# A new begin for two Gram stages: ten pixel groups transposed by TensorE, the centre subtracted behind them, a half step of transfers first

## The chip, the cores and the metric

The kernel runs on one core of a Trainium2 chip. The metric is the device time of one execution in microseconds (us), as the median of several runs. Smaller is better.

## What is computed

The reference applies two bottleneck layers, one after the other, to x of shape 64 x 1024 x 14 x 14 in float32. Cut to what matters, one layer is:

```python
def _bn(x, gamma, beta):
    mean = jnp.mean(x, axis=(0, 2, 3), keepdims=True)
    var = jnp.var(x, axis=(0, 2, 3), keepdims=True)
    xn = (x - mean) * jax.lax.rsqrt(var + EPS)
    return gamma.reshape(1, -1, 1, 1) * xn + beta.reshape(1, -1, 1, 1)

out = relu(_bn(_conv(x, w1, b1, 1, 0), g1, be1))      # 1x1, 1024 -> 256 channels
out = relu(_bn(_conv(out, w2, b2, 1, 1), g2, be2))    # 3x3, 256 -> 256
out = _bn(_conv(out, w3, b3, 1, 0), g3, be3)          # 1x1, 256 -> 1024
out = softplus(residual_scale)[0] * out
return relu(x + out)
```

The mean and variance of each `_bn` run over all 64 images and 196 pixels, 12544 pixels in all. So a layer needs the statistics of its third convolution before it can finish the first pixel.

## The kernel before

**Layout.** The 256 channels in the middle lie as 128 partitions times 2 slots (`s`). `y_all` holds the output of the second convolution for all 12544 pixels (`NPX`) in SBUF.

**Stages.** A layer (block `b` = 0, 1) runs the first convolution, then the second, then a Gram stage, then the third convolution with the residual. In block 0 the third convolution is interleaved with block 1's first.

**The Gram stage.** The third convolution is linear, so the mean and variance of its 1024 outputs follow from the mean and the matrix of second moments of its 256 inputs. The function `gram` builds that matrix. Products of pixels with pixels need the pixels on the partitions, so each group of 256 pixels (`CH * P`, 49 groups) is first transposed into a tile `zt` (six of them in rotation). Then TensorE multiplies the group with itself: two halves of 128 pixels, four products each, added up in two banks of PSUM (`cp`, `ap`; line L170, as all matmuls). The products of a group are queued on TensorE behind the transposition of the next one.

**Two ways to transpose.** `by_tensor` lets TensorE do it: four passes against the identity into PSUM (L1075), then VectorE copies the result to `zt` (L1082). `by_vector` uses VectorE's transpose of 32x32 blocks (L1089). For that the pixels are first brought into another order by transfers: `spread(k)` moves a step of 1536 pixels (`STEP`) from `y_all` into one of two tiles, `homes`, by twelve transfers of 96 KB (L1067), seven issued by SyncE's queue (SP) and five by GpSimd's (POOL). `stay(k)` copies the four diagonal parts on ScalarE (L333). A step makes six groups. A home can be filled again only when VectorE has read the step in it. In block 0 the first home is the tile `ws`, which later holds the sums of weights.

**What is done to y before.** The second batch norm and its ReLU are applied in place, in pieces, by ScalarE (`norm`, through the helper at L333); one small piece goes to VectorE instead (`norm_vector`, L552 and L554). Then VectorE subtracts a constant of each channel, so that the products stay small (`less`, L1033; `minus_c` holds the negated constant). Both must be over before a group is transposed or a step is moved. The order of ScalarE, VectorE and TensorE is the order of the program wherever `keep_in_program_order` is used, which is so for all that is named here, except for two of the four additions in a `combine`.

**Order before.** `FIRST = 7` groups go through TensorE. Step 0 is moved after the second of them, step 1 after the sixth. Seven steps of six groups by VectorE follow; after step k, `spread(k + 2)` is issued, later pieces are normalized and centred, and `stay(k + 2)` is queued. The dummy matmul `busy(psum, "ax", 1)` behind the first group, and seven of them ahead of the stage, keep TensorE's clock up.

**After the groups.** `combine_w3` (and `combine_w1` in block 0) make sums of weights on VectorE, four additions of 512 columns each (L150 to L153), behind the last group's transposition. `conv3_stats` turns the matrix into the statistics; its tile `q` is its own, and `by_mean` lies in the second home (`spare`).

Of the kernel before, what the change touches and what calls it, by code (L numbers as in the profile page):

```python
# [37 lines left out]
FP = mybir.dt.float32  # L38
AF = mybir.ActivationFunctionType
ALU = mybir.AluOpType  # L40

P = 128
# [13 lines left out]

Q = P // 2

FIRST, LAST = 7, 0
RUN = 3 * P  # L60
STEP = 4 * RUN
STEPS = (NPX - (FIRST + LAST) * CH * P) // STEP

LAG = 14

# [24 lines left out]
def bottlenecks(ctx: ExitStack, tc: tile.TileContext, x, w1s, w2s, w3s, pars, out):  # L90
# [240 lines left out]
    def act(*args, **kw):  # L331

        tc.keep_in_program_order(nc.scalar.activation(*args, **kw))  # L333
# [221 lines left out]

    def conv2(psum, pool, b, par, aff, affine_of, stats):

# [438 lines left out]
    def gram(psum, pool, homes, aff, minus_c, beside):  # L996
# [27 lines left out]
        ):  # L1024
            nc.gpsimd.memset(by[i][here, cols], value)

        head = 3 * CH * P
        start = FIRST * CH * P
        bounds = [0, CH * P, head, head + STEP, *range(2 * GPX, NPX + 1, GPX)]
        pieces = list(zip(bounds, bounds[1:]))  # L1030

        def less(s, y):
            tc.keep_in_program_order(nc.vector.tensor_scalar(y, y, minus_c[:, s : s + 1], None, ALU.add))  # L1033

        def norm_to(end):

            while pieces and pieces[0][0] < end:
                a, e = pieces.pop(0)
                for s in reversed(range(MS)):
                    y = y_all[:, s, a:e]  # L1040
                    if a == 0 and s == 1:
                        norm_vector(s, y, aff, minus_c[:, s : s + 1])
                    else:
                        norm(s, y, aff, act)
                        less(s, y)

        def home(k):
            return homes[k % 2][:, : MS * STEP].rearrange("p (s j f) -> p s j f", s=MS, j=4)

        def first_of(k):  # L1050
            return start + k * STEP if k else head

        def stay(k):

            for i in range(4):
                here, a = slice(32 * i, 32 * i + 32), first_of(k) + i * RUN
                act(home(k)[here, :, i], y_all[here, :, a : a + RUN], AF.Copy)

        def spread(k):

            first = first_of(k)
            norm_to(first + STEP)
            x = home(k)
            for n, (i, j) in enumerate(itertools.permutations(range(4), 2)):
                queue = nc.gpsimd if n in (1, 3, 6, 8, 10) else nc.sync
                a = first + i * RUN
                queue.dma_start(out=x[32 * i : 32 * i + 32, :, j], in_=y_all[32 * j : 32 * j + 32, :, a : a + RUN])  # L1067
            return x.rearrange("p s j f -> p (s j) f")

        def by_tensor(a):  # L1070
            tp = psum.tile(CH * M)
            for c in range(CH):
                for s in range(MS):
                    tc.keep_in_program_order(
                        nc.tensor.transpose(  # L1075
                            tp[:, (c * MS + s) * P : (c * MS + s + 1) * P],
                            y_all[:, s, a + c * P : a + (c + 1) * P], ident,
                        )
                    )
            zt = next(zts)  # L1080
            tc.keep_in_program_order(
                nc.vector.tensor_copy(zt[:, :, 1 : M + 1], tp.rearrange("p (c m) -> p c m", c=CH))  # L1082
            )
            return zt

        def by_vector(x, i):
            zt = next(zts)
            tc.keep_in_program_order(
                nc.vector.transpose(  # L1089
                    zt[:, :, 1 : M + 1].rearrange("p b (n c) -> p b n c", c=32),  # L1090
                    x[:, :, i * CH * 32 : (i + 1) * CH * 32].rearrange("p n (b r) -> p b n r", r=32),
                )
            )
            return zt

        def pairs():

            norm_to(head)
            then = {
                1: lambda: ready.append(spread(0)),  # L1100
                2: lambda: (norm_to(2 * GPX), stay(0)),
                4: partial(norm_to, 3 * GPX),
                5: lambda: (ready.append(spread(1)), stay(1)),
            }
            for i in range(FIRST):
                a = i * CH * P
                yield by_tensor(a if a < head else a + STEP)
                if i == 0:
                    busy(psum, "ax", 1)
                if i in then:  # L1110
                    then[i]()
            for k in range(STEPS):
                x = ready.pop(0)
                for i in range(RUN // (CH * 32)):
                    yield by_vector(x, i)
                if k + 2 < STEPS:
                    ready.append(spread(k + 2))
                    norm_to(first_of(k + 2) + 2 * STEP)
                    stay(k + 2)
            norm_to(NPX)  # L1120
            for i in range(LAST):
                yield by_tensor(NPX - (LAST - i) * CH * P)

        ready = []
# [22 lines left out]
    def conv3_stats(psum, one, grams, w3, mv, tags, spare):  # L1147
# [277 lines left out]
    for b in range(2):  # L1425
# [7 lines left out]
        with tc.tile_pool(name=f"last_{b}", bufs=1) as one, tc.tile_pool(  # L1433
            name=f"last_x_{b}", bufs=4 if b == 0 else 5
        ) as xpool:
            w3 = load_w3(one, b)
            if b == 0:
                w1 = load_w1(one, b + 1, nc.sync)
            aff = affine(aggregate(stats2, 0), pb, G2, BE2)
            with ExitStack() as scope:  # L1440
                if b == 0:
                    psum = Psum(scope, ["cy", "ay", "cx", "cy", "ay"], cy=2, ay=2)
                else:
                    psum = Psum(scope, ["cy", "cx"], cy=2, cx=2, cp=2)
                with tc.tile_pool(name=f"gram_{b}", bufs=1) as pool:
                    def x_tile(name):
                        return xpool.tile([P, CS * PX], FP, tag="x", name=name)


                    ws = sums_tile(one, 2 - b)  # L1450
                    homes = [x_tile("home") if b else ws.rearrange("p i n -> p (i n)"), x_tile("home")]

                    weights = []

                    def combined():
                        if b == 0:
                            weights.append(combine_w1(w1, ws[:, 1]))
                        weights.append(combine_w3(w3, ws[:, 0]))

                    beside = {FIRST + STEPS * RUN // (CH * 32): combined}  # L1460
                    grams = gram(psum, pool, homes, aff, minus_c, beside)

                    made = [conv3(psum, 0, 0, w3, "cx" if b else "ay")]
                    mv3 = small.tile([P, CS, nc.vector.BN_AGGR_DIM], FP, tag="mv3", name="mv3")
                    conv3_stats(psum, pool, grams, w3, mv3, ("cy", "cp", "cy", "cp" if b else "cx"), homes[1])
                made.append(conv3(psum, 0, 1, w3, "cx" if b else "ay"))
                if b == 1:
                    made += [conv3(psum, 0, o, w3, tag) for o, tag in zip(range(2, 6), ("cy", "cp") * 2)]
                aff = affine(mv3, pb, G3, BE3, conv_bias=B3)
                for a in aff:  # L1470
                    nc.vector.tensor_scalar(a, a, sps[b], None, ALU.mult)
                xs = [load_x(xpool, b, t) for t in range(2 if b == 0 else 5)]
                residual(psum, xs[0], b, 0, w3, aff, made)
                with tc.tile_pool(name=f"rest_{b}", bufs=1) as pool:
# [46 lines left out]
```

## Time and profile before

| | us |
|---|---|
| median of 3 runs | 1939.28 (1939.04 to 1939.3) |
| the profiled execution | 1940.6 |
| its span, first to last instruction | 1938.8 |
| Gram stage of block 0, first transposition to end of the last product | 587.73 to 655.3 |
| Gram stage of block 1, likewise | 1550.46 to 1618.9 |
| transposition by TensorE, four passes | 0.66 |
| copy of it to `zt` on VectorE | 0.68 |
| transposition of a group by VectorE | 0.67 |
| subtraction of the constant, 1536 columns | 1.01 |
| norm of 1536 columns on ScalarE | 1.65 |
| a home's copy on ScalarE, one of four | 0.84 |
| transfer into a home, from issue to landing, median | 3.4 |

How to read it: times of single instructions are durations; on one engine the next instruction of such a kind may start some 0.1 us before the end of the last. The profiled execution is one run, with the profiler on. PE is TensorE, DVE is VectorE, ACT is ScalarE, POOL is GpSimd, SP is SyncE's queue of transfers. "L1033" is a line of the kernel. In the lists of waits, "A <- B" says that A's engine stood idle until B was done.

### The profile page before, as it was taken

What the parts mean: (1) busy time and instruction counts of PE and PEld (TensorE: products, weight loads), DVE (VectorE), ACT (ScalarE), POOL (GpSimd) and SP (SyncE); (2) the same over time, 40 slices, a digit from 0 to 9 for tenths busy, and PEclk for the clock granted to TensorE, in tenths of its full rate; (3) what the DMA queues carried; (4) which work ended last, traced back from release to release, by engine and by line L of the source; (5) the groups of instructions that cost most, each with busy time, mean ns of one, the idle gap of its engine ahead of it and who ended that gap; (6) DMA issues with size and microseconds to landing.
All of it is one profiled execution on the core that took longest, in us unless ns stands there. A gap on an engine that the chain in (4) does not pass through costs nothing. (4 is left out here: it accounts for less than half of the span.)

```text
span 1938.8 us, 28681 instructions
## 1 busy us (share of the span) xinstructions
PE 1906.2 (98%) x10230; PEld 1599.6 (83%) x10230; DVE 1547.2 (80%) x2479; ACT 1093.2 (56%) x2154; POOL 565.0 (29%) x672
## 2 busy tenths in 40 slices
PE   9999999999998999999999999999999989999999
PEld 5555557999996799999999999989999977555555
DVE  5778767999998767676776767689999976888886
ACT  2222214677778255555555555457777692666666
POOL 0111100211204133333434334302121041666664
PEclk9999999999999999999999999999999999999999
DMA  7777634787946534444444444258788455899998
GB/s 288 274 247 269 231 133 158 201 223 202 227 147 163 187 146 187 167 166 175 180 179 167 166 183 180 104 182 212 213 210 223 141 146 226 285 330 340 331 337 304
DMA packets 198271, 408.51 MB, mean 211 GB/s; under 512 B 36912, under 2 KB 174864, under 8 KB 181616
## 3 DMA queue, kind: packets, MB, share of 16 engines
q1 hardware_dynamic: 159488, 321.91, 48.6%
q0 software_dynamic: 33024, 33.70, 8.4%
q10 hardware_dynamic: 5616, 51.06, 6.3%
q8 instruction: 81, 1.33, 0.3%
q14 instruction: 62, 0.51, 0.1%
HBM read 263.75 MB, written 115.34 MB: 196 GB/s over the span
## 5 line engine op out<-in xcount | busy, mean ns | idle before, releaser
L333 ACT ACTIVATE cu<-cy,scale 128x196 f32<-128x196 f32 (+1 forms) x552 | 256.9, 474 | 277.8 <-PE cy L170 272.5
L170 PE MATMUL columns<-v,ub 128*128 128x224 f32 (+1 forms) x1536 | 300.7, 337 | 0.0
L333 ACT ACTIVATE x<-x,shift 128x392 f32<-128x392 f32 x428 | 241.0, 613 | 59.6 <-POOL x L492 52.9
L170 PEld LDWEIGHTS columns<-v,ub 128*128 128x128 f32 x1536 | 269.3, 188 | 2.8
L466 DVE SCALAR_TENSOR_TENSOR x<-cp,scale,x 128x196 f32<-128x196 f32 (+1 forms) x368 | 178.0, 484 | 98.1 <-PE cp L170 96.4
L170 PE MATMUL cy<-ct,ws 128*128 128x196 f32 (+1 forms) x736 | 221.9, 383 | 1.1 <-ACT cu L333 1.1
L487 POOL TENSOR_TENSOR x<-x,cu 128x196 f32<-128x196 f32 (+1 forms) x184 | 159.4, 867 | 172.0 <-ACT cu L333 162.5
L170 PE MATMUL ay<-at,ws 128*128 128x196 f32 (+1 forms) x752 | 209.1, 381 | 0.0
L492 POOL TENSOR_TENSOR x<-x,cu 128x392 f32<-128x392 f32 x124 | 125.8, 1014 | 192.9 <-DVE x L466 188.2
L170 PEld LDWEIGHTS ay<-at,ws 128*128 128x128 f32 x752 | 136.5, 190 | 33.4
L170 PEld LDWEIGHTS cy<-ct,ws 128*128 128x128 f32 x736 | 133.3, 190 | 36.4 <-ACT cu L333 4.4
L170 PE MATMUL l<-diffs,ub 128*128 128x224 f32 (+1 forms) x768 | 149.2, 337 | 2.6 <-PE columns L170 2.6
L513 POOL TENSOR_TENSOR x<-x,cu 128x392 f32<-128x392 f32 x120 | 121.9, 1017 | 86.9 <-DVE x L466 72.2
L170 PE MATMUL m<-sums,ua 128*128 128x224 f32 (+1 forms) x752 | 145.9, 337 | 1.1 <-DVE sums L624 1.1
L333 ACT ACTIVATE au<-ay 128x196 f32<-128x196 f32 (+1 forms) x141 | 53.8, 381 | 156.7 <-PE ay L170 153.9
L170 PEld LDWEIGHTS l<-diffs,ub 128*128 128x128 f32 x768 | 134.3, 189 | 4.5 <-PE columns L170 3.9
L466 DVE SCALAR_TENSOR_TENSOR x<-cx,scale,x 128x196 f32<-128x196 f32 (+1 forms) x184 | 89.0, 484 | 57.5 <-PE cx L170 57.5
L170 PEld LDWEIGHTS m<-sums,ua 128*128 128x128 f32 x752 | 131.3, 189 | 2.9 <-DVE sums L624 2.5
L170 PE MATMUL cx<-y,w 128*128 128x196 f32 (+1 forms) x404 | 124.2, 393 | 0.4 <-DVE x L1202 0.4
L170 PE MATMUL cy<-y,w 128*128 128x196 f32 (+1 forms) x404 | 123.8, 392 | 0.0
L170 PE MATMUL cp<-y,ws 128*128 128x196 f32 (+1 forms) x368 | 113.6, 390 | 1.5 <-DVE x L466 1.4
L760 ACT ACTIVATE columns<-m 128x448 f32<-128x448 f32 (+1 forms) x160 | 78.4, 490 | 59.8 <-PE m L170 57.3
(216 smaller groups left out, 3977.1 us busy)
## 6 DMA issues: line engine op xcount, KB each, us to landing
x<-in_x SPq DMA_DIRECT2D x62, 1568.0 KB, 6.9
ub<-u SPq DMA_DIRECT2D x94, 768.0 KB, 5.6
x<-mid SPq DMA_DIRECT2D x32, 1568.0 KB, 8.3
mid<-x ACTq DMA_DIRECT2D x31, 1568.0 KB, 5.1
out<-x SPq DMA_DIRECT2D x123, 392.0 KB, 5.5
ua<-u SPq DMA_DIRECT2D x94, 256.0 KB, 3.2
u<-y POOLq DMA_DIRECT2D x48, 256.0 KB, 5.7
home<-y SPq DMA_DIRECT2D x70, 96.0 KB, 3.4
```

The source lines that it names most:

```text
L170: tc.keep_in_program_order(nc.tensor.matmul(*args, **kw))
L333: tc.keep_in_program_order(nc.scalar.activation(*args, **kw))
L466: nc.vector.scalar_tensor_tensor(v, bank, self.scale[:, o : o + 1], v, ALU.mult, ALU.add)
L487: nc.gpsimd.tensor_add(self.part(1, 1), self.part(1, 1), u3)
L492: nc.gpsimd.tensor_add(v, v, self.u12)
L513: nc.gpsimd.tensor_add(v, v, self.u12[:, i * self.n : (i + 1) * self.n])
L760: nc.scalar.activation(v, m, AF.Copy)
```

## The change

Ten groups go through TensorE instead of seven: 4, 3 and 3 (`still`), taken from between the pieces that are moved (`moved`): first half a step (768 pixels, three groups), then six steps. The constant isn't subtracted from y ahead of these ten. Instead it is made into a row, `c_row`, by two matmuls against the identity and a copy on ScalarE ahead of the stage's first norm, and added while the transposed group goes from PSUM to `zt`. The subtraction from y itself, which the third convolution still needs, comes later (`rest`), beside steps 2 to 4. The half step and the first step are moved with their diagonal parts (16 transfers each, nine by SP and seven by POOL, no `stay`); the first step's transfers are issued in two halves. Subtractions for step k + 2 stand between the transposes of step k, behind its second and fourth group, and the norms and copies have a written order. One piece of the norm on VectorE becomes three, in two instructions each, and the two for the last of the ten groups are spread over two groups. `combine_w3` moves behind group 44 of 0 to 48, that is behind the second group of the last step, and `combine_w1` behind group 47. `q` moves into the second home.

The diff, cut where nothing but names change:

```diff
-FIRST, LAST = 7, 0
-STEPS = (NPX - (FIRST + LAST) * CH * P) // STEP
+STEPS = (NPX - 10 * CH * P) // STEP
...
-    def norm_vector(s, y, aff, less=0.0):
+    def norm_vector(s, y, aff):
         scale, shift = aff
-        tc.keep_in_program_order(
+        yield tc.keep_in_program_order(
             nc.vector.tensor_scalar(y, y, scale[:, s : s + 1], shift[:, s : s + 1], ALU.mult, ALU.add)
         )
-        tc.keep_in_program_order(nc.vector.tensor_scalar(y, y, 0.0, less, ALU.max, ALU.add))
+        yield tc.keep_in_program_order(nc.vector.tensor_scalar(y, y, 0.0, None, ALU.max))
...
+        px = CH * P
+        both = tuple(reversed(range(MS)))
+        pieces = 4 * px, STEP // 2, 3 * px, STEP, 3 * px, *[STEP] * (STEPS - 1)
+        bounds = list(itertools.accumulate(pieces, initial=0))
         pieces = list(zip(bounds, bounds[1:]))
...
+        still, moved = pieces[0:5:2], [*pieces[1:5:2], *pieces[5:]]
+        def normed(a, e, slots=both):
+            for s in slots:
+                norm(s, y_all[:, s, a:e], aff, act)
+        def less(a, e, slots=both):
+            for s in slots:
+                y = y_all[:, s, a:e]
+                tc.keep_in_program_order(nc.vector.tensor_scalar(y, y, minus_c[:, s : s + 1], None, ALU.add))
         def home(k):
+            a, e = moved[k]
+            x = homes[(k + 1) % 2][:, : MS * (e - a)].rearrange("p (s j f) -> p s j f", s=MS, j=4)
+            return x, a, (e - a) // 4
...
+        def move(k, runs=range(4)):
+            x, a, run = home(k)
+            for i, j in itertools.product(runs, range(4)):
+                if k > 1 and i == j:
+                    continue
+                n = 4 * i + j if k < 2 else 3 * i + j - (j > i)
+                queue = nc.gpsimd if n in ((1, 3, 6, 8, 10, 13, 15) if k < 2 else (1, 3, 6, 8, 10)) else nc.sync
+                queue.dma_start(
+                    out=x[32 * i : 32 * i + 32, :, j], in_=y_all[32 * j : 32 * j + 32, :, a + i * run : a + i * run + run]
+                )
+        c_row = pool.tile([P, M], FP, tag="c_row", name="c_row")
+        def center_row():
+            ps = psum.tile(M, "ax")
+            for s in range(MS):
+                matmul(
+                    ps[:, s * P : (s + 1) * P], minus_c[:, s : s + 1].to_broadcast([P, P]), ident, start=True, stop=True
+                )
+            act(c_row, ps, AF.Copy)
         def by_tensor(a):
...
-                nc.vector.tensor_copy(zt[:, :, 1 : M + 1], tp.rearrange("p (c m) -> p c m", c=CH))
+                nc.vector.tensor_add(
+                    zt[:, :, 1 : M + 1], tp.rearrange("p (c m) -> p c m", c=CH), c_row[:, None, :].to_broadcast([P, CH, M])
+                )
...
+            def later():
+                for step in norm_vector(1, y_all[:, 1, slice(*still[2])], aff):
+                    yield step
+            center_row()
+            for a in 0, px:
+                for _ in norm_vector(1, y_all[:, 1, a : a + px], aff):
+                    pass
+                normed(a, a + px, (0,))
+            normed(2 * px, 4 * px)
+            starts = [a for piece in still for a in range(*piece, px)]
+            first, second = parts(moved[1])
+            by_steps = later()
+            for n, a in enumerate(starts):
+                yield by_tensor(a)
+                if n == 0:
                     busy(psum, "ax", 1)
+                    normed(*moved[0])
+                elif n == 1:
+                    less(*moved[0], both[:1])
+                elif n == 2:
+                    less(*moved[0], both[1:])
+                    move(0)
+                    normed(*still[1])
+                elif n == 3:
+                    normed(*first)
+                    normed(*still[2], (0,))
+                    normed(*second)
+                elif n == 4:
+                    next(by_steps)
+                elif n == 5:
+                    less(*first)
+                    move(1, range(2))
+                    normed(*moved[2])
+                elif n == 6:
+                    next(by_steps)
+                elif n == 7:
+                    less(*second)
+                    move(1, range(2, 4))
+                elif n == 8:
+                    less(*moved[2], both[:1])
+            normed(*moved[3])
+            rest = [(piece, s) for piece in still for s in range(MS)]
+            for k, (a, e) in enumerate(moved):
+                ahead = k + 2 if k else 2
+                for i in range((e - a) // px):
+                    yield by_vector(k, i)
+                    if k == 0:
+                        if i == 0:
+                            less(*moved[2], both[1:])
+                    elif i in (1, 3) and k + 2 < len(moved):
+                        less(*moved[k + 2], both[i // 2 : i // 2 + 1])
+                    elif i in (0, 5) and k > 1 and rest:
+                        piece, s = rest.pop(0)
+                        less(*piece, (s,))
+                if k + 2 < len(moved):
+                    move(k + 2)
+                    if k and k + 3 < len(moved):
+                        normed(*moved[k + 3])
                     stay(k + 2)
...
-        q = one.tile([P, MS, C], FP, tag="q", name="q")
+        q = spare[:, C : 3 * C].rearrange("p (s n) -> p s n", s=MS)
...
-                    beside = {FIRST + STEPS * RUN // (CH * 32): combined}
+                    beside = {NPX // (CH * P) - 5: lambda: made_c.append(combine_w3(w3, ws[:, 0]))}
+                    if b == 0:
+                        beside[NPX // (CH * P) - 2] = lambda: made_a.append(combine_w1(w1, ws[:, 1]))
```

In the prediction T0 to T9 are the ten transpositions on TensorE, step 0 is the half step and steps 1 to 6 are the whole ones of the new order.

More of the change, by code (lines that the diff above doesn't have):

```diff
@@ L1025, in gram @@
             nc.gpsimd.memset(by[i][here, cols], value)
-        head = 3 * CH * P
-        start = FIRST * CH * P
-        bounds = [0, CH * P, head, head + STEP, *range(2 * GPX, NPX + 1, GPX)]
+        px = CH * P
+        both = tuple(reversed(range(MS)))
+        pieces = 4 * px, STEP // 2, 3 * px, STEP, 3 * px, *[STEP] * (STEPS - 1)
+        bounds = list(itertools.accumulate(pieces, initial=0))
         pieces = list(zip(bounds, bounds[1:]))
-        def less(s, y):
-            tc.keep_in_program_order(nc.vector.tensor_scalar(y, y, minus_c[:, s : s + 1], None, ALU.add))
@@ L1035, in norm_to @@
[L1035 to L1045, printed above, removed]
+        still, moved = pieces[0:5:2], [*pieces[1:5:2], *pieces[5:]]
+        def normed(a, e, slots=both):
+            for s in slots:
+                norm(s, y_all[:, s, a:e], aff, act)
@@ L1047, in home @@
+        def less(a, e, slots=both):
+            for s in slots:
+                y = y_all[:, s, a:e]
+                tc.keep_in_program_order(nc.vector.tensor_scalar(y, y, minus_c[:, s : s + 1], None, ALU.add))
         def home(k):
-            return homes[k % 2][:, : MS * STEP].rearrange("p (s j f) -> p s j f", s=MS, j=4)
-        def first_of(k):
-            return start + k * STEP if k else head
+            a, e = moved[k]
+            x = homes[(k + 1) % 2][:, : MS * (e - a)].rearrange("p (s j f) -> p s j f", s=MS, j=4)
+            return x, a, (e - a) // 4
@@ L1053, in stay @@
         def stay(k):
+            x, a, run = home(k)
             for i in range(4):
[L1056 to L1068, printed above, removed]
+                here = slice(32 * i, 32 * i + 32)
+                act(x[here, :, i], y_all[here, :, a + i * run : a + i * run + run], AF.Copy)
@@ new lines, in move @@
+        def move(k, runs=range(4)):
+            x, a, run = home(k)
+            for i, j in itertools.product(runs, range(4)):
[6 more added lines that the diff above has]
+                )
@@ L1081, in by_tensor, with by_vector @@
             tc.keep_in_program_order(
-                nc.vector.tensor_copy(zt[:, :, 1 : M + 1], tp.rearrange("p (c m) -> p c m", c=CH))
-            )
-            return zt
-        def by_vector(x, i):
-            zt = next(zts)
+                nc.vector.tensor_add(
+                    zt[:, :, 1 : M + 1], tp.rearrange("p (c m) -> p c m", c=CH), c_row[:, None, :].to_broadcast([P, CH, M])
+                )
+            )
+            return zt
+        def by_vector(k, i):
+            zt, x = next(zts), home(k)[0].rearrange("p s j f -> p (s j) f")
             tc.keep_in_program_order(
@@ L1096, in pairs @@
         def pairs():
[L1098 to L1108, printed above, removed]
-                    busy(psum, "ax", 1)
-                if i in then:
-                    then[i]()
@@ L1112, in pairs, with parts @@
[L1112 to L1118, printed above, removed]
+            def parts(piece):
+                (a, e), mid = piece, sum(piece) // 2
+                return (a, mid), (mid, e)
+            def later():
+                for step in norm_vector(1, y_all[:, 1, slice(*still[2])], aff):
+                    yield step
@@ L1119, in pairs @@
                     stay(k + 2)
[L1120 to L1124, printed above, removed]
+            assert not rest
         total = NPX // (CH * P)
@@ L1451, in bottlenecks @@
                     homes = [x_tile("home") if b else ws.rearrange("p i n -> p (i n)"), x_tile("home")]
[L1453 to L1458, printed above, removed]
-                    beside = {FIRST + STEPS * RUN // (CH * 32): combined}
+                    made_c, made_a = [], []
+                    beside = {NPX // (CH * P) - 5: lambda: made_c.append(combine_w3(w3, ws[:, 0]))}
+                    if b == 0:
+                        beside[NPX // (CH * P) - 2] = lambda: made_a.append(combine_w1(w1, ws[:, 1]))
                     grams = gram(psum, pool, homes, aff, minus_c, beside)
@@ L1473, in bottlenecks @@
                 residual(psum, xs[0], b, 0, w3, aff, made)
+                weights = made_a + made_c
                 with tc.tile_pool(name=f"rest_{b}", bufs=1) as pool:
```

## The prediction, made before the changed kernel was run

> **What bounds the kernel now.** I read the page first: how busy each engine is, then the slices.
>
> ```profile
> span 1938.8 us, 28681 instructions
> PE 1906.2 (98%) x10230; PEld 1599.6 (83%) x10230; DVE 1547.2 (80%) x2479; ACT 1093.2 (56%) x2154; POOL 565.0 (29%) x672
> ```
>
> TensorE (PE) is busy for 98%, so only what it waits for, or what it need not do, can be won. The two Gram stages lie at 588 to 655 us (block 0) and 1550 to 1619 us (block 1). Next, the windows of 2 us in block 1's stage: columns are the stretch, its length, busy time of PE, PE loads, DVE, ACT, POOL, the clock, the DMA share and GB/s.
>
> ```profile
> 1556.00:1558.00 2.00, 0.87 (x8) 0.69 (x10) 1.18 (x3) 1.95 (x4) 2.00 (x4) 1.00 0.51 114
> 1562.00:1564.00 2.00, 0.70 (x12) 0.41 (x8) 1.45 (x3) 2.00 (x2) 0.00 (x0) 1.00 0.04 13
> 1566.00:1568.00 2.00, 0.23 (x4) 0.22 (x6) 1.93 (x3) 1.95 (x4) 1.75 (x3) 1.00 1.00 244
> 1576.00:1578.00 2.00, 0.41 (x6) 0.38 (x8) 2.00 (x3) 1.95 (x3) 0.00 (x0) 1.00 0.81 186
> 1580.00:1582.00 2.00, 2.00 (x18) 1.78 (x16) 1.53 (x2) 2.00 (x2) 0.85 (x1) 0.50 0.10 24
> ```
>
> PE stands still four times in the first 27 us, and then runs for a while at half clock. Who it waits for, in the waits of the same stage (total, times, longest):
>
> ```profile
> PE cp L170 <- DVE zt L1089: 1.9, 1, 1.9
> PE cp L170 <- DVE zt L1082: 1.8, 1, 1.8
> PE cx L1075 <- DVE y L1033: 1.6, 1, 1.6
> PE cy L1075 <- DVE y L1033: 1.4, 1, 1.4
> ```
>
> All four end with VectorE (DVE): twice a transposition waits until the centre has been subtracted (L1033), twice the products wait for a `zt` that is queued behind such subtractions. Last, DVE's timeline late in that stage, which prices the loop of the transfers:
>
> ```profile
> 1590.10 3.67 DVE L1089 STREAM_TRANSPOSE zt<-home 128x512 f32<-128x512 f32 x6
> 1596.54 3.68 DVE L1089 STREAM_TRANSPOSE zt<-home 128x512 f32<-128x512 f32 x6 [2.77 <-ACT home L333]
> 1601.33 1.93 DVE L1089 STREAM_TRANSPOSE zt<-home 128x512 f32<-128x512 f32 x3 [1.11 <-ACT home L333]
> ```
>
> Six DVE transposes take 3.67 us, 0.595 each after the first. Step 3 of the old seven (0 to 6) ends at 1593.77 and its home is refilled for step 5 at 1601.33: 7.6 us from the last read to the first read of new data (the label names ACT, whose copies ended at 1597.3; the last transfer landed at 1600.8). I call this time D. The six refills that DVE waited for took 8.6, 7.4 and 8.0 (block 0), 9.4, 7.6 and 8.1 (block 1). PE needs no `zt` late here, since DVE runs 2 to 4 us ahead of it.
>
> **Removed: the stalls.** Centre subtraction leaves the path of the first groups. By PE's timeline the idle stretches are 1.63, 1.38, 1.80 and 1.92 us in block 1, and 1.62, 1.38, 1.80, 1.93 and 0.49 in block 0: 6.73 and 7.22. Behind block 1's last one the clock was granted at one half for 3.41 us, worth 1.7. Together 15.65 us, all on the path, and the most that can be won.
>
> The Trainium skill, page "TensorE: Matmul & The Clock Gate", section "HAM oscillation — how this bites in real kernels", warns only of idle gaps above some 3.4 us; this trace shows half clock behind 1.92 us, and none behind 1.93 us in block 0, so the measurement decides. By that rule the 1.7 would not belong to these gaps, and the sum below would be 1.7 smaller.
>
> **Added on PE.** Transposed groups follow each other every 1.835 us (594.39, 596.23, 598.06), groups from DVE every 1.10. Three more per stage cost 3 x 0.735 = 2.2, and 4.4 in both. All of it is on the path.
>
> [...]
>
> **Added at the begin: the row of centres.** Its passes stand behind the 14 warming passes, which end at 1549.99 in block 1, and its copy stands first in ACT's order, ahead of all the norms, which before started at 1549.17 and now queue behind it. Four passes of 128 columns: between 0.118 (64 columns, 16 in 1.89) and 0.19 (a weight load) each; I take 0.7 in all. Then ACT's copy (0.38 for 196 columns; 0.33 until the next may start, plus 0.1 to be released), the norm of 256 columns 0.60, and 0.1 to PE: first transposition at 1551.8 instead of 1550.46. Later by 1.35 (1.1 to 1.5), in both 2.7. The subtracting evacuation is nearest to L1182's product from PSUM (128x512, 0.69) against the copy's 0.68: nothing.
>
> **Walking the new begin.** T0 at 1551.8, T1 1.29 later (the dummy lies between), then one every 1.835, T6 at 1562.27. T7 needs the second half of the DVE norm, queued behind T6's evacuation: 1563.03 + 0.60 + 0.61 + 0.1 = 1564.34 instead of 1564.10, so 0.23, and 0.46 in both. Everything else is covered. ACT normalizes a 768-column piece every 0.9 us and is two pieces ahead. The half step is issued at 1556.9, behind T2's evacuation and its subtraction: nine on SP at 0.64 and seven on POOL, last landing near 1565, read at 1569.4, a cover of 4 us. The second half of step 1 is issued at 1566.8: four on SP, and 3.4 us median to land, 1572.1 to 1572.7, wanted by 1573.4. Were that cover gone, its lateness would count in full.
>
> Transfers per stage go from 84 to 92 for the same bytes, ACT's home copies from 28 to 20 (0.84 each, off the path). `q` in the spare home lets the fifth x load start 1.8 us later; nobody wants it for some 20 us. Without that cover it costs 1.8.
>
> **The new loop.** Now each DVE step carries two subtractions of 1536 columns (0.93) and, in steps 2 to 4, a late one of 768 or 1024 in front (0.52, 0.65 between the rows of 832 and 1536). A step takes DVE 5.9 to 6.1 instead of 3.6, and its home is free only then. Two steps of PE take 13.17, a loop 6.0 + D. With D = 7.7 it takes 13.7. T9 falls on 1568.01, its evacuation on 1568.77, the first transpose of step 0 on 1569.37; with one subtraction and two more transposes step 0's home is read by 1572.17. PE multiplies group 9 from 1569.84 (0.585 for T9's passes, 1.25 for group 8) and wants step 1 four groups later at 1574.23, step 2 six later at 1580.82. Step 2 starts at 1572.17 + 7.7 = 1579.87, and 0.79 later (0.69, and 0.1 to PE) its first `zt` is there, 1580.66: in time by 0.16. Its third group waits behind late subtraction, transpose, subtraction: 2.76 against PE's 2.2, late by 0.41 after that 0.16. By the same walk step 4 is late by 0.12 at its first and 0.41 at its third group, step 6 by 0.13 at its first. Then combine_w3 stands behind step 6's second group: four adds of 0.61, so the third group is late by 1.44; in block 0 combine_w1 makes the last late by 0.95 more. That is 2.51 and 3.46. Two of each four adds aren't held in order; if they move back, 1.29 and 1.29. I take the middle, 1.9 + 2.4 = 4.3.
>
> D is the open size. The four refills of the last two steps of each block, beside few norms, average 7.75; all six have a median of 8.0. I take 7.7, since the new moves of steps 5 and 6 run beside an ACT without norms too. Each 0.1 more costs 0.6 (three places, two stages).
>
> **The sum.** 15.65 - 4.4 - 2.7 - 0.46 - 4.3 = 3.8 us. The profiled execution took 1940.6 (span 1938.8 and 1.8 around it), 1.3 above the median 1939.28; taken off the median, 1935.5.
>
> **Rivals.** All covered: refills as fast as 7.0 (the shortest transfer) and DVE ahead at the combines. Then the 4.3 stay won: 8.1 us, 1931.2. For it: before, step 6 was 3 to 4 us ahead. Against: DVE then had no subtractions inside the steps.
>
> The stalls come back as late `zt`: D of 8.0 to 8.2 and the combines whole. At 8.2: 8.1 - 6.0 - 3.0 = -0.9, at 8.0 with the middle +2.0; 1937.3 to 1940.2, no difference that counts. For it: the median of the six. The change then does not do what it says, since the waits only move from the begin to the steps.
>
> Slower: transfers beside a DVE that never pauses are as slow as the slowest, D = 9.4 in steps 2, 4 and 6. 1.7 x 6 = 10.2 more: 3.8 - 10.2 = -6.4, 1945.7. It decides from D = 8.3, and beyond 0.2% from 9.0. For it: packets of 1536 B took 65 ns (median) where DVE waited, 107 where it worked. Against: one of six.
>
> **How the numbers follow.** 0.2% is 3.9 us, about what a measurement of this kernel can tell from no change. Forecast case (2 to 6 us won, its middle on the bound) 0.42, of which 0.24 beyond it and 0.18 within; all covered 0.22, faster; late `zt` 0.23, within; slower 0.13. Faster 0.24 + 0.22 = 0.46, same 0.18 + 0.23 = 0.41, slower 0.13. The range reaches from the full gain of 8.1 and 1.2 us more (short waits of PE under 0.05 us, not counted above, may go too) to 1.3 us beyond the third case's slow end: 1930.0 to 1941.5. It leaves out most of the slower case and the edges.
>
> **What would show it.** Right: first transposition 1.8 us after the last warming pass; ten transposed groups every 1.835 with only T7 late; no half clock; PE waits of some 0.4 at third groups of steps 2 and 4 and of 0.2 to 1.4 behind the combine. From the last warming pass to the Gram's end 68.05 becomes 66.9 (block 0), 68.91 becomes 66.1 (block 1). Wrong: step 1 landing after 1573.4, a stretch at half clock, refills outside 7.0 to 8.3, or a DVE that is groups ahead at step 6.

## The result, and the profile after

The changed kernel takes 1946.07 us (median of 6 runs, 1944.79 to 1947.18), the kernel before 1939.13 beside it: ratio 1.0036, with a 95% interval of 1.0023 to 1.0049. It is slower by 0.36%, where 1935.5 was forecast. Its profiled execution took 1945.16 us. First the page: span, then busy time by engine.

```profile
span 1943.4 us, 28801 instructions
PE 1912.6 (98%) x10262; PEld 1601.7 (82%) x10262; DVE 1548.5 (80%) x2493; ACT 1081.4 (56%) x2148; POOL 565.7 (29%) x680
```

PE is busy 6.4 us longer than before. Who it waits for in block 0's Gram stage (total, times, longest):

```profile
PE cp L169 <- DVE zt L1099: 7.7, 2, 6.9
PE cy L1083 <- ACT y L332: 1.0, 1, 1.0
```

and in block 1's:

```profile
PE cp L169 <- DVE zt L1099: 2.7, 5, 1.3
PE cy L1083 <- ACT y L332: 1.0, 1, 1.0
```

The stops that ended with a subtraction (L1033 before) are gone from both. In their place block 0 has one stop of 6.9 us and one of 0.8, block 1 five short ones. VectorE's timeline shows where the long one is: three transposes of step 0 (home), then 8.20 us of waiting for a transfer, then step 1 (ws).

```profile
607.44 1.30 DVE L1099 STREAM_TRANSPOSE zt<-home 128x512 f32<-128x512 f32 x2
616.94 1.30 DVE L1099 STREAM_TRANSPOSE zt<-ws 128x512 f32<-128x512 f32 x2 [8.20 <-DMA home<-y]
```

The label goes by the last landing ahead of this read, that of a transfer of step 2 into `home` at 616.8. What VectorE needed was step 1 in `ws`, and its last transfer landed at 616.2. So step 1 came late. SP's timeline over the transfers that should bring it:

```profile
597.69 2.50 SPq L1063 DMA_DIRECT2D home<-y  x3
600.24 0.59 SPq L124 DMA_DIRECT2D x<-in_x  x1
600.93 9.24 SPq L1063 DMA_DIRECT2D ws<-y  x9
```

Between the half step (home) and step 1 (ws) stands a load of x, the first input of block 0's residual. Before, and in block 1 after, all such loads stood behind the last step's transfers. The program names it after the Gram stage, but the written order that the text ahead of the prediction speaks of is held for ScalarE, VectorE and TensorE alone: nothing holds the transfers' order on SP, and the load needs nothing that isn't there early. What it did to its neighbours, by issues of the same stretch (KB each, median us from issue to landing):

```profile
x<-in_x SPq DMA_DIRECT2D x1, 1568.0 KB, 8.7
ws<-y SPq DMA_DIRECT2D x9, 96.0 KB, 8.7
ws<-y POOLq DMA_DIRECT2D x7, 96.0 KB, 7.8
```

Step 1's transfers take 8.7 and 7.8 us instead of 3.4 and 3.1 (e1 below), on POOL's queue too. The Trainium skill says why the second queue is no way around, page "DMA: Bandwidth & Descriptors", section "Issuing engines are not separate DMA queues": transfers of all issuing engines run on the same 16 DMA engines and interleave. The trace agrees: packets of 12544 B, 0.59 us each by the median, held these engines from 601.6 to 607.9. The load did one thing more. By SP's waits of this stretch (total, times, longest), SP stood until it had landed, at 608.9:

```profile
SPq L1063 <- DMA x<-in_x: 2.3, 1, 2.3
```

The load and the transfer that SP issued behind this wait signal their landing on the same semaphore, one of eight that SP uses in turn. The last two transfers of step 1 were issued only then, at 608.9 and 609.6, and they landed last; all others of step 1 had landed by 614.7. How much of the lateness is this hold and how much the bytes, no run separates. Last, PE and its clock in windows of 2 us (length, busy PE, PE loads, DVE, ACT, POOL, clock, DMA share, GB/s):

```profile
612.00:614.00 2.00, 0.00 (x0) 0.00 (x0) 0.00 (x0) 1.97 (x3) 0.00 (x0) 1.00 1.08 264
614.00:616.00 2.00, 0.00 (x0) 0.00 (x0) 0.00 (x0) 1.46 (x1) 0.00 (x0) 0.88 1.04 250
616.00:618.00 2.00, 0.29 (x2) 0.29 (x4) 1.06 (x2) 0.00 (x0) 0.00 (x0) 0.50 0.81 174
618.00:620.00 2.00, 2.00 (x18) 1.66 (x17) 2.00 (x4) 0.00 (x0) 0.00 (x0) 0.50 0.05 14
620.00:622.00 2.00, 2.00 (x18) 1.69 (x16) 2.00 (x4) 0.00 (x0) 0.00 (x0) 0.50 0.01 4
```

PE stands from 610.82 to 617.71, and the clock is at half for 6.8 us, from 615.5 to 622.4. In PE's timeline, half pace cost 2.3 us: the starts of the next groups lie 2.20, 2.15 and 1.25 us apart instead of 1.10.

Block 1, where no load slipped forward, ran nearly as forecast up to step 1: first transposition 1.80 us behind the last warming pass, no wait at T7, step 1 landed 21.06 us behind the first transposition (forecast 20.3 to 20.9).

### The profile page after: what moved, and what is told of

It reads as the page before. It is cut to its first block, busy times and chain, and to the rows that moved or that the text cites. A ratio compares the mean times of both kernels' runs of the same rounds, so it can differ in the third digit from the quotient of the medians.

```text
span 1943.4 us, 28801 instructions
## 1 busy us (share of the span) xinstructions
PE 1912.6 (98%) x10262; PEld 1601.7 (82%) x10262; DVE 1548.5 (80%) x2493; ACT 1081.4 (56%) x2148; POOL 565.7 (29%) x680
## 4 chain that ended last, share of the span: by engine, by line
PE 91%; DVE 4%; DMA 1%; issue 1%; ACT 1%; POOL 1%; SPq 0%; DVEq 0%; ACTq 0%; POOLq 0%
PE cy L169 17%; PE ay L169 17%; PE columns L169 13%; PE cp L169 11%; PE ap L169 10%; PE m L169 7%; PE l L169 6%; PE cx L169 5%; PE ax L169 5%; PE ps L169 1%; DMA home<-y 1%; DMA ws<-y 0%; DVE zt L1099 0%; SPq L1063 0%; POOL home L1063 0%
## 5 line engine op out<-in xcount | busy, mean ns | idle before, releaser
L169 PE MATMUL cp<-zt 128*64 128x193 f32 x784 | 102.3, 335 | 10.5 <-DVE zt L1099 10.4
```

Of the source, the lines that this page charges most:

```text
L169: tc.keep_in_program_order(nc.tensor.matmul(*args, **kw))
```

## The experiments

Sixteen kernels, all built on the changed one but e12. Each ratio is to the kernel before, run beside it.

| kernel | us, median | ratio to before, 95% interval |
|---|---|---|
| changed | 1946.07 | 1.0036, 1.0023 to 1.0049 |
| e1 load held behind | 1940.02 | 1.0005, 0.9996 to 1.0013 |
| e7 half the load early | 1943.62 | 1.0025, 1.0016 to 1.0034 |
| e12 before, load early | 1939.81 | 1.0004, 0.9995 to 1.0013 |
| e6, e9 changed, stop filled | 1947.07, 1946.24 | 1.0041, 1.0025 to 1.0056; 1.0035, 1.0023 to 1.0047 |
| e5 = e1, banks' turn back | 1938.81 | 0.9999, 0.9990 to 1.0008 |
| e2 = e1, combines early | 1937.62 | 0.9991, 0.9983 to 1.0000 |
| e3 = e1, row's copy later | 1938.21 | 0.9995, 0.9986 to 1.0004 |
| e4 = e1, e2, e3 | 1935.85 | 0.9983, 0.9974 to 0.9991 |
| e8 = e4, e5 | 1934.70 | 0.9977, 0.9968 to 0.9985 |
| e11 = e8, late subtractions moved | 1934.66 | 0.9977, 0.9968 to 0.9986 |
| e10 = e8, even queues | 1941.71 | 1.0013, 1.0004 to 1.0022 |
| e13 = e10, loads held in block 1 too | 1937.34 | 0.9990, 0.9981 to 0.9999 |
| e14 = e8, late subtractions on ACT, loads held in block 1 too | 1934.48 | 0.9980, 0.9971 to 0.9989 |
| e15 = e14, combine_w1 last | 1932.84 | 0.9966, 0.9953 to 0.9978 |
| e16 = e15, own centre for block 1 | 1931.73 | 0.9957, 0.9943 to 0.9970 |

### The load

e1 pins it:

```diff
-            nc.sync.dma_start(
+            (tc.keep_in_program_order if behind else id)(nc.sync.dma_start(
...
-                xs = [load_x(xpool, b, t) for t in range(2 if b == 0 else 5)]
+                xs = [load_x(xpool, b, t, behind=b == 0) for t in range(2 if b == 0 else 5)]
```

> The changed kernel with one thing held: in block 0 the first load of x for the residual (1568 KB, issued on SP at 600.24 in the changed kernel, between the half step's transfers and step 1's) is kept behind the last step's transfers, where it stood before the change. SP's order is the only thing that differs. Theory (the load fills the transfer engines ahead of step 1): step 1 lands by 611, the PE gap of 6.89 us in front of its products goes, and the half clock of 6.8 us behind it (worth 3.4) with it; 1946.1 - 6.9 - 3.4 = 1935.8 us, between 1934.5 and 1937. Rival A (step 1's sixteen transfers are themselves too slow in block 0): the gap stays above 4 us, time 1943 or more. Rival B (the time is lost in the later steps, in subtractions and combines): about 1945 to 1946.

Measured 1940.02: 6.05 us came back, not the 10.3 expected of the stop and the clock. SP's timeline and block 0's waits of PE:

```profile
597.55 3.94 SPq L1063 DMA_DIRECT2D home<-y  x4
601.59 5.77 SPq L1063 DMA_DIRECT2D ws<-y  x9
```

```profile
PE cp L169 <- DVE zt L1099: 3.0, 4, 1.3
PE cy L1083 <- ACT y L332: 1.0, 1, 1.0
```

Step 1 landed at 610.2, the long stop and the half clock are gone; but stops of 0.71, 0.21, 1.27 and 0.80 stand where the changed kernel, being late already, had only 0.11 and 0.80. The load is the largest cause, and not all of it. e7 splits the load in two and pins the second half only:

```diff
+            (tc.keep_in_program_order if behind and i else id)(nc.sync.dma_start(
...
+                xs = [load_x(xpool, b, t, 2 - b if t == 0 else 1, b == 0) for t in range(2 if b == 0 else 5)]
```

> The changed kernel with only the first half of the early load (784 KB) in its place ahead of step 1, the other half behind the last step. If the load costs by its bytes (1568 KB took the engines 6.3 us, 601.6 to 607.9), step 1 lands 3.1 us earlier, the PE gap of 6.89 becomes 3.8, and the time lies midway between the changed kernel (1946.1) and the one with the load held behind (1940.0): 1942 to 1943.5, by what the clock does. Rival (it costs by being in SP's queue, whatever its size): 1946.

The stop was 4.20 us, the time 1943.62, 0.6 above midway. The price grows with the bytes in front, though half of them cost 3.6 of the 6.05; SP stood 1.2 us for this half instead of 2.3. e12 puts the whole load inside step 1's transfers of the kernel before:

```diff
+                if k == 1 and queue is nc.sync:
+                    tc.keep_in_program_order(ins)
+                if k == 1 and n == 2:
+                    early()
```

> The kernel before with the first x load of block 0's residual put behind the second of SP's transfers of step 1, all else in its order. Theory (the load takes the engines 6.3 us, and what it costs is that less the cover of the step behind it): step 1 landed at 609.3 and was read at 614.1, so 4.8 us are covered and about 1.5 come through, 1940.7; with a stretch at half clock 1942 to 1943. Rival (the load costs the 6 us that it cost in the changed kernel wherever it stands in front of a step): 1945.

Measured 1939.81, against 1938.71 for before beside it. PE's longest wait in block 0, in e7 and then in e12:

```profile
PE cp L169 <- DVE zt L1099: 5.0, 2, 4.2
PE cp L170 <- DVE zt L1093: 3.2, 1, 3.2
```

In e12 step 1 was read 1.3 us later and PE's fourth stop grew from 1.93 to 3.21, with no half clock behind it. The same load costs 6 us in one order and about 1 in the other. The old order had 4.8 us to spare, the new one nothing: in e1 VectorE waits 1.1 us for step 1 as it is.

### The half clock

e6 puts nine passes on PE in front of step 1's products in block 0, e9 six:

```diff
+                    elif k == 1 and i == 0 and len(beside) == 2:
+                        busy(psum, "ax", 9)
```

> The changed kernel, its early load left where it is, with nine more passes of 448 columns on PE (some 0.65 us each) in block 0 in front of step 1's products, where PE stands still for 6.89 us. They hold no work of the result. If the half clock from 615.8 to 622.6 comes from the standing still, it goes: PE worked at half pace from 617.7 to 622.6, 4.9 us, so 2.4 us are won, 1943.7, less what late steps take back. Rival (the clock falls for another reason, or PE isn't the bound there): 1946.

> The changed kernel, early load left in place, with six passes of 448 columns in front of step 1's products in block 0; they hold no work of the result. In the run with nine each took 1.08 us, not 0.65, so that they ran 2.6 us past the data; six take 6.5 us and end with the landing. The half clock goes, 2.4 us of half pace with it: 1943.7 if PE is the bound behind the stall; 1946 if what is won there is lost again in later steps.

The passes of e6 took 1.08 us each and ran past the data: its 1947.07 tells nothing of the price. Those of e9 end at 617.22, and the clock stays full. Its windows, and its waits in block 0:

```profile
616.00:618.00 2.00, 1.17 (x3) 0.30 (x2) 0.03 (x1) 0.00 (x0) 0.00 (x0) 1.00 1.06 236
618.00:620.00 2.00, 1.27 (x18) 1.18 (x20) 2.00 (x3) 0.00 (x0) 0.00 (x0) 1.00 0.17 40
620.00:622.00 2.00, 2.00 (x34) 1.85 (x32) 2.00 (x4) 0.00 (x0) 0.00 (x0) 1.00 0.01 4
```

```profile
PE cp L169 <- DVE zt L1099: 3.5, 3, 1.5
```

Yet the time is 1946.24, as before the filling (the profile is of the slowest of six runs, 1947.27). Step 1 was read 1.0 us later behind the first transposition than in the changed kernel, and a stop of 1.25 us stands behind step 6's second group, at combine_w3, where that kernel had 0.11: what PE won in pace it waited for later. From step 1's first transpose to step 6's it took 33.7 us in e9 and 34.0 in the changed kernel, and to the stage's last product 43.8 and 44.1: of the 2.3 us of half pace 0.3 came through. So PE isn't the bound there. Why step 1 was read later in e9 is open.

### The turn of the banks

In e1 PE also stops behind the stage, between 655 and 690 us:

```profile
PE cy L169 <- ACT cu L332: 1.6, 3, 1.0
PE ay L169 <- DVE x L1251: 1.2, 1, 1.2
```

PSUM banks are taken from a list of five in turn. Seven transposed groups left the turn at the third, ten leave it at the first, and the residual then comes upon the bank whose two buffers hold its first two products as the second it takes, instead of the third. e5 turns it back:

```diff
+ grams, _ = gram(psum, pool, homes, aff, minus_c, beside), [next(psum.cycle) for _ in range(2 - b)]
```

> As the kernel with the load held behind, and behind the Gram the turn of the PSUM banks is advanced (two places in block 0, one in block 1) to where it stood before the change. Ten transposed groups instead of seven take three banks more from the turn, so that block 0's residual begins with the two banks that hold its first two products. Theory (the turn): the PE gaps of 1.15 us (669.68, in front of the third product of the residual) and 1.02 us (678.32) in the kernel with the load held go or shrink to the 0.37 to 0.87 that the kernel before shows there (2.77 us in all between 655 and 690 against 1.81 before); 1.0 us less than the kernel with the load held, 1939.0. Rival (the gaps come from the x load or VectorE's order): the same gaps, 1940.

Measured 1938.81, 1.2 less; the waits are those of the kernel before again:

```profile
PE cp L169 <- DVE x L465: 0.9, 1, 0.9
PE cy L169 <- ACT cu L332: 0.5, 2, 0.4
PE cx L169 <- DVE x L1251: 0.4, 1, 0.4
```

### The combines and the begin

The changed kernel's timeline of VectorE at the end of block 1's stage:

```profile
1615.16 1.30 DVE L1099 STREAM_TRANSPOSE zt<-home 128x512 f32<-128x512 f32 x2 [3.95 <-PE ap L169]
1616.39 0.65 DVE L149 TENSOR_TENSOR ws<-w 128x512 f32<-128x512 f32 x1
1617.07 0.69 DVE L150 TENSOR_TENSOR ws<-ws,w 128x512 f32<-128x512 f32 x1
1617.68 0.69 DVE L151 TENSOR_TENSOR ws<-w 128x512 f32<-128x512 f32 x1
1618.29 0.68 DVE L152 TENSOR_TENSOR ws<-w,ws 128x512 f32<-128x512 f32 x1
1618.89 2.48 DVE L1099 STREAM_TRANSPOSE zt<-home 128x512 f32<-128x512 f32 x4
```

VectorE waits 3.95 us for step 6 and then has all four adds between its groups. (The label names PE. But step 6's last transfer landed at 1614.6, and behind it the trace has only VectorE's checks of semaphores, seven in all some 0.1 us apart, up to the read at 1615.16.) e2 moves them into that wait; e3 moves ACT's copy of the row behind the first norm:

```diff
-                    beside = {NPX // (CH * P) - 5: lambda: made_c.append(combine_w3(w3, ws[:, 0]))}
+                    beside = {NPX // (CH * P) - 7: lambda: made_c.append(combine_w3(w3, ws[:, 0]))}
...
-                        beside[NPX // (CH * P) - 2] = lambda: made_a.append(combine_w1(w1, ws[:, 1]))
+                        beside[NPX // (CH * P) - 6] = lambda: made_a.append(combine_w1(w1, ws[:, 1]))
```

> As the kernel with the load held behind, and the combines of the weights stand ahead of the last step's transposes in VectorE's order (combine_w3 behind the last transpose of step 5, combine_w1 behind the first of step 6) instead of between its second and sixth. If the PE gaps at the end of the Gram stages (0.80 in block 0, 1.30 in block 1) are the combines standing in front of a zt, they go, because VectorE waits 3.95 us for step 6's data there anyway: 2 us less than the kernel with the load held, 1933.8 if that is 1935.8. Rival: the last step's data are late by themselves and the combine only fills that wait; then nothing is won, or its 2.6 us (5.2 in block 0) put the first zt off and 1 to 2 us are lost.

```diff
-            act(c_row, ps, AF.Copy)
+            return ps
...
-            center_row()
+            ps = center_row()
...
-                normed(a, a + px, (0,))
+                normed(a, a + px, (0,)), a or act(c_row, ps, AF.Copy)
```

> As the kernel with the load held behind, and ACT's copy of the row of centres stands behind the first norm of slot 0 rather than ahead of it. If the copy in front of the norm is what puts the first transposition off (1.80 us behind the last warming pass instead of 0.46), the transposition starts right behind the row's passes, 0.8 to 1.0 us earlier in each block: 1.6 to 2.0 us less than the kernel with the load held. Rival: the first norms are late for another reason, or the time comes back as a later wait (the evacuation of the first group waits for the row): less than 0.5 us.

> The load held behind, the combines early and the row's copy behind the first norm, all three in one kernel. If they are independent: the kernel with the load held less 2.0 (combines) less 1.8 (row), 1932.0 if that is 1935.8; about 7 us under the kernel before. If the end of the Gram is set by the transfers' loop and not by its begin, the earlier begin comes back as a later wait in front of steps 2, 4 and 6, and it stands no better than the better of the two.

> The load held behind, the combines early, the row's copy behind the first norm, and the turn of the banks as before: the kernel with the first three measured 1935.85 us; with the banks 1.0 less, 1934.8. If the banks make nothing, 1935.9.

e2 won 2.40, e3 1.81, both 4.17, and with the banks 1.15 more: each near what was expected, and they add up. But in block 0 the stops at the end did not go in e2: one of 1.81 us in front of step 6's second group, behind combine_w1, stands in place of the 1.27 and 0.80. e15 below takes this up. In e3 the first transposition starts right behind the row's passes, at 588.30.

### The loop

Left in e8 are stops in and in front of steps 1 to 6 (0.96 us in block 1, 2.6 in block 0). Three tries to shorten what stands before them. e11 has the late subtractions two groups later:

```diff
-                    elif i in (0, 5) and k > 1 and rest:
+                    elif i in (2, 5) and k > 1 and rest:
```

> As the kernel with four changes (1934.7), and the late subtractions of the transposed pieces stand behind the third group of steps 2 to 4 instead of behind the first. If their place is what makes the third groups late (0.42 us between groups' starts, at steps 2 and 4 of each block), these waits go: 0.8 to 1.6 us less, 1933.5. If VectorE is simply full, they move to the fourth groups and nothing is won.

Nothing won: later by two groups within the step, the first of each step's two late subtractions costs the same. The other one was not moved. e10 gives six transfers of a step to each queue, and e13 pins block 1's loads as well:

```diff
-                queue = nc.gpsimd if n in ((1, 3, 6, 8, 10, 13, 15) if k < 2 else (1, 3, 6, 8, 10)) else nc.sync
+                queue = nc.gpsimd if n in ((1, 3, 6, 8, 10, 13, 15) if k < 2 else (1, 3, 5, 7, 9, 11)) else nc.sync
```

> As the kernel with four changes (1934.7), and the twelve transfers of a step go six to SP and six to POOL instead of seven and five. SP issues one every 0.64 us, and the last one lands 2.4 to 3.5 us behind its issue; if SP's seventh issue sets a refill (D, 8.0 us median), D falls by about 0.6 us, the waits in front of steps 2, 4 and 6 shrink with it, and 1 to 2 us are won: 1933.2. If the transfer engines' rate sets D (their share is 0.8 to 1.0 in those windows), D stays at 8.0 and the time at 1934.7.

This run leaves its question open. SP's timeline in block 1 shows the first cause again, loads of x ahead of steps 2 and 4:

```profile
1573.88 0.92 SPq L1063 DMA_DIRECT2D home<-y  x1
1574.86 0.58 SPq L124 DMA_DIRECT2D x<-mid  x1
1577.92 13.96 SPq L1063 DMA_DIRECT2D home<-y  x12
1591.92 0.88 SPq L124 DMA_DIRECT2D x<-mid  x1
```

> As the kernel with even queues (six transfers of a step on SP, six on POOL), and the x loads are kept behind the transfers in block 1 too: with even queues two of them (issued at 1574.86 and 1591.92) had slipped in front of steps 2 and 4 there. Theory: those two loads were the whole loss against the kernel with four changes (1941.7 against 1934.7); without them 1934.7, since even in block 0, where none slipped, a refill took 8.1, 8.8, 8.8, 9.0 and 7.8 us with even queues, no less than with seven and five (7.5, 7.9, 8.4, 8.9, 7.8). Rival (SP's seventh issue sets a refill): 1933 or less. Rival (POOL's sixth transfer slows it): 1937 or more.

Without those loads 1937.34: they cost 4.4 us, and even queues cost 2.6 against seven and five. The refills took 8.5 us (mean of ten) instead of 8.1. So sparing SP its seventh issue didn't shorten them; why a sixth transfer on POOL makes them longer is open. e14 takes VectorE's late subtractions to ACT, in steps 5 and 6, and holds block 1's loads as e13 does (in e8 they already stood behind the last step's transfers):

```diff
-                    elif i in (0, 5) and k > 1 and rest:
+                    elif i in (0, 2, 4) and k > 4 and rest:
                         piece, s = rest.pop(0)
-                        less(*piece, (s,))
+                        act(y_all[:, s, slice(*piece)], y_all[:, s, slice(*piece)], AF.Identity, bias=minus_c[:, s : s + 1])
```

> As the kernel with four changes (1934.7; the loads held in both blocks), and the six late subtractions of the transposed pieces of each block run on ACT during steps 5 and 6 instead of on VectorE in steps 2 to 4. Theory (the end of a Gram stage is set by the loop of VectorE's step, 6.1 us, and a refill, 8.0, three times 14.1 = 42.3 against TensorE's 39.6): steps 2 to 4 take VectorE 5.5 instead of 6.1, the even chain is 1.2 us shorter, and the waits in front of step 6 (2.0 us of lateness in block 0, 0.6 in block 1) shrink: 1 to 2 us less, 1933.2. Rival (TensorE is the bound, what waits are left are single accidents): nothing, 1934.7. Moving these subtractions two groups later within the steps had won nothing (1934.66).

The median is 1934.48 (1932.61 to 1938.06), no gain that counts, but the stages moved apart. In block 1 step 6 begins 34.5 us behind step 1 instead of 35.2 (TensorE needs 33.0 for these 30 groups), and the stage, from the first transposition to the last product, takes 63.6 us instead of 64.2. The 34.5 stands clear of the others: in the eleven profiles with seven and five transfers and the late subtractions on VectorE it is 35.1 to 35.9. Block 0 lost it again, at combine_w1 and in a wait that e15 shows. (e14's profile is of a run of 1937.4, 3 us above the median, with half clock in block 0.) e15 puts combine_w1 behind the last transpose:

```diff
-                        beside[NPX // (CH * P) - 6] = lambda: made_a.append(combine_w1(w1, ws[:, 1]))
+                        beside[NPX // (CH * P) - 1] = lambda: made_a.append(combine_w1(w1, ws[:, 1]))
```

> As the kernel with the late subtractions on ACT, and in block 0 combine_w1 (four adds, 2.6 us) stands behind the last transpose of step 6 instead of behind its first. If the wait of 1.79 us in front of step 6's second group in block 0 is this combine, it goes, and nothing takes its place, since TensorE has two groups (2.2 us) and two products of the residual in hand there: 1 to 1.8 us less than that kernel, 1931.8. If the scaling of the Gram behind it waits for the combine: no gain.

Measured 1932.84, 1.6 less. VectorE there:

```profile
641.64 0.68 DVE L152 TENSOR_TENSOR ws<-w,ws 128x512 f32<-128x512 f32 x1
644.48 0.17 DVE L1477 TENSOR_SCALAR minus_c<-par 128x2 f32<-128x2 f32 x1 [2.16 <-ACT y L332]
645.08 3.68 DVE L1099 STREAM_TRANSPOSE zt<-home 128x512 f32<-128x512 f32 x6 [0.43 <-issue]
```

Block 1's `minus_c` is written into the tile that ACT still reads, ahead of step 6. In e16 each block has its own columns:

```diff
+    centres = keep.tile([P, 2, MS], FP, tag='minus_c', name='minus_c')
...
-        minus_c = keep.tile([P, MS], FP, tag="minus_c", name="minus_c")
+        minus_c = centres[:, b]
```

> As the kernel with combine_w1 last (1932.8), and each block has its own columns for the negative centre. In that kernel block 1's centre was written into the tile that block 0's late subtractions on ACT still read: VectorE waited 2.16 us for ACT (642.3 to 644.5) with this small write standing in front of step 6's first transpose, whose data had landed at 642.7 and were read at 645.1. Theory: the wait goes, and the PE gap of 1.84 us in block 0 (644.0) with it, 1931.0. Rival (another wait, the last transfer or the combine, takes its place): 1932.8.

```profile
644.86 0.68 DVE L152 TENSOR_TENSOR ws<-w,ws 128x512 f32<-128x512 f32 x1
645.46 3.67 DVE L1099 STREAM_TRANSPOSE zt<-home 128x512 f32<-128x512 f32 x6
```

The wait is gone and PE doesn't stop in front of step 6 in block 0; the time is 1931.73 (5 runs, 1929.2 to 1933.2; e15 1932.2 to 1933.1), so this last gain is not settled. The refills of block 0 were slower in this profile (8.8 to 9.0 in steps 3 to 5) and left stops of 0.8 to 1.0 in front of steps 1, 3 and 5. It has the lowest median of all: 7.5 us under the kernel before.

## Why the prediction was wrong

**The step that failed: the walk of the new begin.** It put step 1's landing at 1572.1 to 1572.7 and its need at 1573.4, and wrote that without this cover "its lateness would count in full". It was walked for block 1 only, with the queue taken to hold what the program names there. In block 0 there were 1568 KB more in front. It looked at a load of x once, for the fifth of block 1, and took SP's order to be as fixed as VectorE's and ACT's: it never asked what could pass the moved transfers. This cost 6.05 us (e1). "Step 1 landing after 1573.4" and "a stretch at half clock" stood among the signs of an error, and both came, in block 0.

**Left out: the banks' turn**, 1.2 us (e5). Three more groups were counted by their passes and not by what they take from a list that others draw on.

**Under-sized: the new loop**, put at 4.3 us, measured 8.5. In e1 the starts of groups behind T9 lie 8.5 us (4.25 and 4.24) farther apart than 1.10 each. Its terms: D measured 8.0 (mean of ten, 7.1 to 8.7) instead of 7.7, 1.8 us by the prediction's own 0.6 for each 0.1; combine_w3 was late in full (1.52) and combine_w1 by 0.97, where the middle was taken, 1.7 us. Together 4.3 + 1.8 + 1.7 = 7.8 of the 8.5. The rival "late `zt`" had these sizes, D of 8.0 to 8.2 and the combines whole. The rival "slower" named 1945.7, close to the 1946.07, but by refills of 9.4; in e1 none took more than 8.7. That its number came near is chance.

**Right.** The three added groups (every 1.835), the later begin (1.34 in each block, 1.35 forecast; e3 took 1.81 of the two back), and the stops removed. These were worth 1.5 us more than their idle time, since the groups behind a stop start up to 0.2 us farther apart. The wait at T7 (0.46) didn't come. So in e1 the Gram stages won 15.65 + 1.5 - 4.4 - 2.7 - 8.5 = 1.6; measured from the last warming pass, 0.39 + 1.31 = 1.7.

**The account.** Forecast to result is 10.6 us: 6.05 (load), 1.2 (banks) and 4.2 (loop) lost, 1.5 and 0.46 won back, 9.5 in all. The other 1.1 is not closed: e1 should stand 0.5 us under the kernel before, its profiled span is 1.0 lower and its median 1.0 higher, and runs of one kernel spread over 2 to 3 us.

**The bound.** The first part said that TensorE bounds the kernel. Inside the changed stages VectorE's step of 6.1 us and a refill of 8.0 make 14.1 for two steps, against TensorE's 13.2. The prediction had computed this loop (13.7) but treated its excess as single waits on PE's path; in e9, with the half clock gone, only 0.3 of 2.3 us came through while the loop was behind; in e14 and e15, with a shorter loop (steps 2 to 4 take VectorE 5.6 us), block 1's five steps are 0.7 to 1.1 us shorter. This is read from their profiles; e14's median alone doesn't show it.

## What to carry to other kernels

A fixed order of the compute engines isn't a fixed order of the transfers: ask of every queue what could be issued early there, and pin the large loads behind the small transfers that somebody waits for. A stop that is taken away is worth only what the next bound leaves, so compare the period of the loop that feeds the engine (step plus refill) with the engine's own before pricing the gain. And count what a moved or added step takes from shared rings and tiles, PSUM banks and small constants too.

## What the runs showed of the hardware that was not expected

- A load of 1568 KB delayed transfers of 96 KB on the other queue nearly as much as on its own: 7.8 and 8.7 us to land, against 3.1 and 3.4 in e1. On its own queue it also held two issues back, by 2.3 us.
- Half clock followed stops of 6.89 and 4.20 us, beginning 4.7 and 2.2 us into them, and not the one of 3.21 in e12; but also 1.92 in the kernel before, and in e14's profile two stops of 1.83 and 1.81 with 1.3 us of work between, where it began inside the second. The Trainium skill, page "TensorE: Matmul & The Clock Gate", section "HAM oscillation — how this bites in real kernels", gives gaps above some 3.4 us: the first three agree, the last two do not. Nor does the length of a single short stop decide: 1.93 in block 0 of the kernel before and 1.83 in e15 had no half clock behind them.
- Each pass of 448 columns in e6 and e9 took 1.08 us, where 0.65 had been read from the gap that the single one leaves between the first two transpositions.
